# Two loads of W_v, and the normalisation of the last three tiles of x, moved earlier in a Strassen-blocked graph attention kernel

## The chip, the cores and the metric

One core of a Trainium2 chip runs the whole program. The metric is the device time of one execution in microseconds (us), and lower is better. The kernel before takes 630.65 us (median of three runs, 630.48 to 630.88). PE is the matrix engine, DVE the vector engine, ACT the scalar engine, POOL the GpSimd engine; SP issues most of the transfers. ACT and POOL issue transfers too.

## The reference, cut to what matters

The input has 2708 nodes with 1024 features, and a 0/1 adjacency matrix with about four ones in a row.

```
h = relu(layernorm(x))
q = h @ W_q.T + b_q;  k = h @ W_k.T + b_k;  v = h @ W_v.T + b_v
z = (q @ k.T) / 32 * adj;  z = where(z == 0, -10000, z)
out = x + relu(softmax(z, axis=1) @ v)
```

Everything is float32.

## The kernel before

**What is computed.** A row's scores are needed only where adj has a one. The program folds W_q and W_k into one matrix M of 1024x1024, forms a row q' = h M for each node, and takes the scalar products of q' with the few rows of h that adj names. The weighted sum u of these rows of h goes through W_v last: out = x + relu(u W_v.T + b_v). A rare general path (from L1397 on) is compiled but not run here.

**Stages.** (1) To about 104 us PE forms M. Meanwhile tiles of 128 rows of x are loaded, normalised and stored as `h_dram`, and DVE searches tiles of adj for their ones. (2) Ten "q pairs" (two row tiles each) are multiplied by M. Tiles 0 to 7, the early ones, are still in SBUF in their natural order. From tile 8 on the rows are gathered in an order sorted by number of neighbours; this needs the sorted table `tab` and all of `h_dram`. (3) The attention stream gathers neighbours' rows of h (`g`), multiplies them with q' on DVE (L863) and sums them (L923), tile after tile, beside stage 2 and 4. (4) Ten "o pairs" and one lone tile of u are multiplied by W_v.

**One pair.** A pair's product goes by Strassen's scheme in 512x512 blocks: seven products of eight matmuls each (`add_block`, L1010). The weights are M's four blocks, `M[:, i, j]`, and four combinations of them, `T[:, 0..3]`, which lie in the tile `wlow`. `multiply(n)` runs the pair's products with calls of `after(0)` to `after(6)` between them. All other work is issued from `after`. Between `after(5)` and the last product of pair n stands `between(n)`, which calls `opened(n + 1)`: it issues the first two products of the next pair, X with the weights `M[:, 0, 0]` (copied on to the bank Y by ACT at L1023) and Z with `T[:, 0]` for a q pair or `M[:, 0, 1]` for an o pair. So each pair is opened one pair ahead.

**From M to W_v.** With the last q pair (index 9, `last_q`) the weights change. Each block may be overwritten once its last q product has run. `b11` is `M[:, 0, 0]`, `t1` is `M[:, 0, 1]`, `b21` is `M[:, 1, 0]`. B11 of W_v goes to `M[:, 0, 0]`, and B22 to `T[:, 0]`, from where ACT copies it to `M[:, 1, 1]` (L1274) and where DVE takes it for `T[:, 1]` (L1282). The first o pair's X product needs B11.

**The early tiles' steps.** Strings of short steps, put at places (n, i) of `after` by the table `steps_at`, order the work of stage 2: `s8-10` loads x of tiles 8 to 10 and takes their moments on DVE (L237, L238), `r8` makes scale and shift of the three on POOL (nine small instructions, L259 to L267), `a8` normalises on ACT (L276), `k8` stores them to `h_dram` from ACT's queue (L283). `p` counts a tile of adj on ACT (L368), `f` searches one on DVE (L389), `w8-14 w15-21` writes the sorted table on POOL (L626), `z` reads it back (L638). At (2, 5) POOL adds tiles 8, 9 and 10 to `hsum` (L298, `owe`) and gathers the rows of the next two pairs (L612, tile `qr`). DVE and ACT run in the order in which the program issues, and POOL does so in this stretch.

**Queues.** Each engine issues its transfers in its own order, and an instruction that waits holds up all behind it on that engine.

Of the kernel before, what the change touches and what calls it, by code (L numbers as in the profile page):

```python
# [65 lines left out]
def tile_preln_masked_attention(  # L66
# [12 lines left out]
    nc = tc.nc  # L79
# [120 lines left out]
    M = core.tile([P, 2, 2, 4, NB], FT, name="M")  # L200
# [108 lines left out]
    def follow(steps):  # L309

        for step in steps.split():
            first, *only = step[1:].split(".")
            first, *last = first.split("-")
            first = int(first or 0)
            if step[0] == "s":
                stats(range(first, int(last[0] if last else first) + 1))
            elif step[0] == "m":
                moments(first)
            elif step[0] == "r":
                root(first)  # L320
            elif step[0] == "a":
                apply(first, *[range(int(o[0]), int(o[-1]) + 1) for o in only])
            elif step[0] in "hk":
                keep(first, step[0] == "h")
            elif step[0] == "+":
                owe(first)
            elif step[0] == "p":
                counted(first)
            elif step[0] == "c":
                counts(*halves[first])  # L330
            elif step[0] == "o":
                sorted_at.append(sort(*halves[first]))
            elif step[0] == "w":
                pooled.close()
                with tc.issue_after((behind if first < EARLY else products)[-1].ins):
                    entered.append(put(first, int(last[0]) + 1))
            elif step == "z":
                pooled.enter_context(tc.manual_schedule(engines={mybir.EngineType.Pool}))
                with tc.issue_after(entered[-1].ins):
                    reload(EARLY, NT)  # L340
            elif step[0] == "b":
                reload(*halves[first])
            elif step[0] == "g":
                squared(first)
            else:
                if step[0] == "e":
                    counted(first)
                if step[0] != "j":
                    found(first, *[range(int(o[0]), int(o[-1]) + 1) for o in only])
                if step[0] != "i":  # L350
                    listed(first)
# [81 lines left out]
    T = wlow.rearrange("p (k a) (b w) -> p k (a b) w", a=2, b=2)  # L433
# [12 lines left out]
    with tc.tile_pool(name="w", bufs=1, side="left") as wp:  # L446
# [11 lines left out]
        t1 = [work.tile([P, D], FT, tag="hT", name=f"t1_{k}", bufs=2) for k in range(2)]  # L458
# [145 lines left out]
    def small(name):  # L604
        return half.tile([P, NB], FT, tag="half", name=name, bufs=14)
# [157 lines left out]
    def natural_rows(n):  # L763
# [17 lines left out]

    steps_at = {(0, 0): "s4-5 p8 e9 +19 +20 +21", (0, 1): "r4 +0 +1 +2 i10.0-1", (0, 3): "p10", (0, 4): "i10.2-3 a4",
# [4 lines left out]
    steps_ahead = {(1, 5): "o1"}  # L787

# [219 lines left out]
    def add_block(bank, a, b, last=True):  # L1008
        for c in range(4):
            mm = nc.tensor.matmul(bank, a[:, c, :], b[:, c, :], start=False, stop=(c == 3), skip_group_check=True)  # L1010
        return mm
# [3 lines left out]
    def opened(n):  # L1015

        if n not in banks_of:
            return
        X, Z = banks_of[n]
        ops = ops_of[n][0]  # L1020
        add_block(X, ops["a11"], M[:, 0, 0])
        Y = psum.tile([P, NB], FT, tag="acc", name="psy")
        nc.scalar.copy(Y, X)  # L1023
        if n == FIRST:
            follow("o0")
        products.append(add_block(Z, ops["s1"], T[:, 0] if units[n][0] == "q" else M[:, 0, 1]))
        p5 = small("p5")
        nc.scalar.copy(p5, Z)
        opened_of[n] = Y, p5

    def between(n):

        if n == len(units) - 1:
            single["first"] = one_started(single["banks"], single["turned"][:, 0:4, :])
        else:
            opened(n + 1)

    def one_started(banks, a):

        X, Z = banks  # L1040
        add_block(X, a, M[:, 0, 0])
        first = small("p_single")
        nc.scalar.copy(first, X)
        return first

    def multiply(n, results, after):


        X, Z = banks_of.pop(n)
        ops = ops_of.pop(n)[0]  # L1050
        Y, p5 = opened_of.pop(n)
        after(0)
        after(1)
        products.append(add_block(Y, ops["s2"], T[:, 1]))
        u2 = small("u2")
        nc.scalar.copy(u2, Y)
        after(2)
        add_block(X, ops["a12"], M[:, 1, 0])
        results[0](X)
        after(3)  # L1060
        products.append(add_block(Z, ops["s4"], M[:, 1, 1]))
        results[2](Z, u2)
        after(4)
        products.append(add_block(Y, ops["s3"], T[:, 2]))
        results[1](Y, p5)
        after(5)
        between(n)
        add_block(Y, ops["a22"], T[:, 3])
        results[3](Y)
        after(6)  # L1070
# [119 lines left out]
    def of_wv(i, j):  # L1190

        return wv[j][:, i * 4:(i + 1) * 4, :]
# [26 lines left out]
    last_q = len(q_pairs) - 1  # L1219
# [13 lines left out]
    for n, unit in enumerate(units):  # L1233
# [15 lines left out]
        def after(i):  # L1249
# [15 lines left out]
                    with tc.issue_after(sorted_at[-1].ins):  # L1265
                        nc.vector.memset(g, 0.0)
            b11, t1, b21, b22 = M[:, 0, 0], M[:, 0, 1], M[:, 1, 0], M[:, 1, 1]
            for at, place, src in (((-2, 0), t1, of_wv(0, 0)), ((0, 0), T[:, 0], of_wv(1, 1)), ((0, 0), b11, of_wv(0, 0)),
                                   ((0, 3), b21, of_wv(1, 0))):
                if (n - last_q, i) == at:  # L1270
                    nc.sync.dma_start(place, src)
            if (n - last_q, i) == (0, 4):
# [302 lines left out]
```

## Time and profile before

| | |
|---|---|
| time, median of 3 | 630.65 us |
| the profiled execution, whole | 635.63 us |
| its span, first to last instruction | 633.9 us |
| PE busy | 623.0 us (98%) |
| DVE / POOL / ACT busy | 525.2 / 370.7 / 291.6 us |
| TensorE clock granted, mean | 0.994 |
| moved by DMA | 182.19 MB, mean 287 GB/s |

The profile is one execution on the chip with every instruction's start and duration. PE is busy nearly throughout, so what it waits for and how fast it is clocked set the time; the other engines matter where PE, or a chain that ends in PE, waits for them.

### The profile page before, as it was taken

The page shows a single profiled execution, that of the slowest core. Times are in us where ns is not written, and L with a number is a line of the kernel's source. Part 1 is how long each engine was busy: PE and PEld are TensorE (multiplying, and loading weights), DVE is VectorE, ACT ScalarE, POOL GpSimd, SP SyncE. Part 2 cuts the span into 40 slices and gives each one's busy share as a digit, 9 for nine tenths or more (in the row PEclk, how much of TensorE's full clock was granted, in tenths as well). Part 3 has the DMA queues.
Part 4 walks back from the last instruction along what each step waited for, and adds up shares of the span by engine and source line. Part 5 has one row for each costly group of instructions (what it writes and reads, how often), then busy time and mean ns, then how long its engine had stood idle before and what let it go on. Part 6 is the DMA issues. An engine that isn't in the chain of part 4 may idle for free.

```text
span 633.9 us, 6066 instructions
## 1 busy us (share of the span) xinstructions
PE 623.0 (98%) x1579; PEld 312.0 (49%) x1579; DVE 525.2 (83%) x1022; ACT 291.6 (46%) x421; POOL 370.7 (58%) x394
## 2 busy tenths in 40 slices
PE   9999999999998999999999989999999999999996
PEld 5777766444444544444444434444444444444442
DVE  5999879898897845899897879998988998988741
ACT  3538985749477372443332333444433324342300
POOL 2639960885766677666543432878566776762241
PEclk9999999999999999999999989999999999999999
DMA  8999997598788469996686999899999999996391
GB/s 333 407 365 316 340 351 301 207 320 307 262 257 337 135 196 369 296 410 191 207 343 197 362 346 305 261 335 318 330 285 344 291 297 307 341 286 172 102 295 71
DMA packets 65089, 182.19 MB, mean 287 GB/s; under 512 B 9960, under 2 KB 20024, under 8 KB 64409
## 3 DMA queue, kind: packets, MB, share of 16 engines
q0 software_dynamic: 26656, 86.02, 43.3%
q1 hardware_dynamic: 31594, 71.53, 32.7%
q10 hardware_dynamic: 6798, 24.20, 9.8%
q8 instruction: 14, 0.23, 0.2%
q14 instruction: 27, 0.21, 0.1%
HBM read 146.70 MB, written 43.36 MB: 300 GB/s over the span
## 4 chain that ended last, share of the span: by engine, by line
PE 96%; DMA 3%; issue 0%; POOL 0%; SPq 0%; DVE 0%; ACT 0%; POOLq 0%
PE ps L1010 44%; PE psy L1010 32%; PE ps_y L476 6%; PE ps_x L476 4%; PE ps_z L476 4%; PE pt L415 3%; DMA M<-in_wv_dram 2%; DMA qr<-h_dram,tab 1%; PE ps_y L511 1%; PE ps_h L1226 0%; PE ps_v L594 0%; DVE y_alone L1391 0%; POOL out_dram L1375 0%; ACT q L1101 0%; POOLq L1397 0%
## 5 line engine op out<-in xcount | busy, mean ns | idle before, releaser
L610 POOL DMA_INDIRECT g<-h_dram,tab x93 | 120.5, 1296 | 62.7 <-ACT u L912 21.7
L1010 PE MATMUL ps<-M,a 128*128 128x512 f32 x320 | 145.8, 599 | 2.0 <-DMA M<-in_wv_dram 2.0
L1010 PE MATMUL psy<-wlow,s 128*128 128x512 f32 x320 | 145.1, 596 | 0.0
L863 DVE SCALAR_TENSOR_TENSOR junk<-g,pq 128x1024 uint8<-128x1024 f32 x92 | 112.4, 1221 | 11.8 <-issue 4.9
L1010 PE MATMUL ps<-M,s 128*128 128x512 f32 x240 | 107.9, 592 | 0.0
L1010 PEld LDWEIGHTS ps<-M,a 128*128 128x128 f32 x320 | 60.4, 192 | 75.4 <-issue 71.2
L1010 PEld LDWEIGHTS psy<-wlow,s 128*128 128x128 f32 x320 | 60.6, 192 | 72.9 <-issue 71.9
L923 DVE SCALAR_TENSOR_TENSOR u<-g,coef,u 128x1024 f32<-128x1024 f32 x70 | 89.7, 1281 | 5.5 <-ACT u L912 4.0
L389 DVE FIND_INDEX8 at<-ones,adj 128x8 uint32<-128x685 f32 (+1 forms) x88 | 74.5, 865 | 0.0
L1010 PEld LDWEIGHTS ps<-M,s 128*128 128x128 f32 x240 | 45.5, 190 | 57.2 <-issue 56.5
L1010 PE MATMUL psy<-wlow,a 128*128 128x512 f32 x160 | 71.9, 592 | 0.0
L368 ACT ACTIVATE sized<-adj 128x2708 uint8<-128x2708 f32 (+1 forms) x22 | 54.2, 2465 | 7.9 <-DMA adj<-in_adj_dram 6.6
L1111 POOL DMA_INDIRECT y<-in_x_dram,tab x19 | 34.6, 1821 | 35.6 <-ACT y L1128 24.2
L298 POOL TENSOR_TENSOR hsum<-hsum,x 128x256 f32<-128x256 f32 (+1 forms) x56 | 38.8, 738 | 25.5 <-DVE wlow L444 21.4
L1010 PEld LDWEIGHTS psy<-wlow,a 128*128 128x128 f32 x160 | 30.4, 190 | 38.3 <-issue 37.1
L808 POOL DMA_INDIRECT out_dram<-y,tab x21 | 27.0, 1287 | 19.2 <-issue 13.1
L1010 PE MATMUL ps<-wlow,s 128*128 128x512 f32 x80 | 36.0, 593 | 0.0
L944 ACT COPY v<-u 128x1024 f32<-128x1024 f32 x19 | 19.8, 1044 | 29.1 <-DVE u L923 25.8
L760 ACT COPY ps<-bp_sb 128x512 f32<-128x512 f32 x42 | 24.6, 595 | 10.3 <-DVE y L1146 9.7
L626 POOL DMA_INDIRECT tab_dram<-tab,pos_i x22 | 21.7, 985 | 11.2 <-DVE pos_i L689 5.7
L276 ACT ACTIVATE x<-x,r 128x1024 f32<-128x1024 f32 (+1 forms) x22 | 25.8, 1232 | 5.2 <-POOL r L266 5.2
L912 ACT ACTIVATE u<-g,coef 128x1024 f32<-128x1024 f32 x16 | 18.4, 1149 | 21.3 <-DVE coef L911 13.2
(253 smaller groups left out, 843.4 us busy)
## 6 DMA issues: line engine op xcount, KB each, us to landing
adj<-in_adj_dram SPq DMA_DIRECT2D x21, 1354.0 KB
x<-in_x_dram SPq DMA_DIRECT2D x21, 512.0 KB
h_dram<-x ACTq DMA_DIRECT2D x21, 512.0 KB
u_dram<-v ACTq DMA_DIRECT2D x19, 512.0 KB
or<-u_dram SPq DMA_DIRECT2D x76, 128.0 KB
q_late<-q SPq DMA_DIRECT2D x12, 512.0 KB
pq<-q_late POOLq DMA_DIRECT2D x12, 512.0 KB
M<-in_wv_dram SPq DMA_DIRECT2D x3, 1024.0 KB
```

The source lines that it names most:

```text
L276: nc.scalar.activation(xs[i][:n], xs[i][:n], AF.Relu, bias=r[:n, 4, i:i + 1], scale=r[:n, 3, i:i + 1])
L298: small.append(nc.gpsimd.tensor_add(hsum[:n, cols], hsum[:n, cols], xt[:n, cols]))
L368: nc.scalar.activation(sized[:n], a[:n, :, :PW], AF.Abs, accum_out=total[:n, t:t + 1])
L389: nc.vector.max_index(at[:n, k - first_k, g, :], ones[:n, 0:8], a[:n, g, :])
L476: mm = nc.tensor.matmul(bank, a_tile(o + H * a[0], a[1], i), b(o), start=first and o == 0, stop=(o == H - 1), skip_group_check=True)
L610: return nc.gpsimd.indirect_dma_start(out=dst, out_offset=None, in_=src, in_offset=off, bounds_check=N - 1, oob_is_err=False)
L760: nc.scalar.copy(return_[h], row[:, h * NB:(h + 1) * NB])
L808: to = nc.gpsimd.indirect_dma_start(out=out, out_offset=bass.IndirectOffsetOnAxis(ap=ptab.bitcast(U32)[:n, t, SLOTS:SLOTS + 1], axis=0), i ...
L863: chained(lambda: nc.vector.scalar_tensor_tensor(junk, g_of[t][s], 1.0, tq[t], op0=ALU.mult, op1=ALU.mult, accum_out=zall[:, t, s:s + 1]))
L923: chained(lambda: nc.vector.scalar_tensor_tensor(u, g_of[t][s], coef[:, s:s + 1], u, op0=ALU.mult, op1=ALU.add))
L1010: mm = nc.tensor.matmul(bank, a[:, c, :], b[:, c, :], start=False, stop=(c == 3), skip_group_check=True)
L1111: return nc.gpsimd.indirect_dma_start(out=y[:n], out_offset=None, in_=x, in_offset=off, compute_op=ALU.add)
```

## The change

Two edits. **First**, B22 and B11 of W_v are loaded right behind `opened(last_q)`, in `between(last_q - 1)`, in place of `after(0)` of the last q pair, and B22 goes ahead of B11 as it did. **Second**, in `steps_at` the moments and the root of tiles 8 to 10 (`s8-10 r8`) go from (1, 5) to a place of their own, (1, 4), and their normalisation and stores (`a8 k8`) from (2, 3) to the head of (1, 5). No instruction is added or taken out.

```diff
                 (0, 5): "f11 p11 k4 s6-7", (0, 6): "+3 +4 f12 m6 m7", (1, 1): "p12 f13 c1 r6 +5", (1, 2): "p13",
-                (1, 3): "a6 k6 p14", (1, 5): "s8-10 w8-14 r8 w15-21 f14 f15", (1, 6): "f16 p15", (2, 1): "f17",
-                (2, 2): "p16", (2, 3): "p17 a8 k8 z", (2, 4): "p18", (2, 5): "f18 f19", (2, 6): "p19 f20 p20",
+                (1, 3): "a6 k6 p14", (1, 4): "s8-10 r8", (1, 5): "a8 k8 w8-14 w15-21 f14 f15", (1, 6): "f16 p15", (2, 1): "f17",
+                (2, 2): "p16", (2, 3): "p17 z", (2, 4): "p18", (2, 5): "f18 f19", (2, 6): "p19 f20 p20",
...
         else:
             opened(n + 1)
+        if n == last_q - 1:
+            nc.sync.dma_start(T[:, 0], of_wv(1, 1))
+            nc.sync.dma_start(M[:, 0, 0], of_wv(0, 0))
...
-            for at, place, src in (((-2, 0), t1, of_wv(0, 0)), ((0, 0), T[:, 0], of_wv(1, 1)), ((0, 0), b11, of_wv(0, 0)),
-                                   ((0, 3), b21, of_wv(1, 0))):
+            for at, place, src in (((-2, 0), t1, of_wv(0, 0)), ((0, 3), b21, of_wv(1, 0))):
                 if (n - last_q, i) == at:
                     nc.sync.dma_start(place, src)
```

SP's queue around the loads of W_v, in pairs 8 and 9, before (`wlow` is the tile of `T`, `or` the first o pairs' rows, `q_late` the store of q' of tiles 8 to 19):

```order
L1086 DMA q_late<-q_2152 128x1024
L700 DMA or_2258<-u_dram 32x4x256 x4
L700 DMA or_2263<-u_dram 32x4x256 x4
L1086 DMA q_late<-q_2153 128x1024
L1271 DMA wlow<-in_wv_dram 128x2048
L1271 DMA M<-in_wv_dram 128x2048 x2
L700 DMA or_2370<-u_dram 32x4x256 x4
```

and of the change:

```order
L1089 DMA q_late<-q_2152 128x1024
L700 DMA or_2258<-u_dram 32x4x256 x4
L700 DMA or_2263<-u_dram 32x4x256 x4
L1038 DMA wlow<-in_wv_dram 128x2048
L1039 DMA M<-in_wv_dram 128x2048
L1089 DMA q_late<-q_2153 128x1024
L1273 DMA M<-in_wv_dram 128x2048
L700 DMA or_2370<-u_dram 32x4x256 x4
```

B22 and B11 now stand ahead of the store of q' of tile 17; B21 stands where it stood.

DVE in pair 1, around the sort of the table (L682 to L689; `x_1110` and the two after it are tiles 8 to 10, which the change numbers `x_1094`, `x_1100`, `x_1106`), before:

```order
L1096 TENSOR_TENSOR q_992<-ps_880,u_1048 128x512
L1093 TENSOR_TENSOR q_993<-psy,p_957 128x512
L682 COPY sort<-ps_all 128x252
...
L689 CAST pos_i<-deg 128x14
L237 BN_STATS st<-x_1110 128x6 x2
L238 BN_AGGR mv<-st 128x2
L237 BN_STATS st<-x_1116 128x6 x2
L238 BN_AGGR mv<-st 128x2
L237 BN_STATS st<-x_1122 128x6 x2
```

and of the change:

```order
L1099 TENSOR_TENSOR q_992<-ps_880,u_1048 128x512
L237 BN_STATS st<-x_1094 128x6 x2
L238 BN_AGGR mv<-st 128x2
L237 BN_STATS st<-x_1100 128x6 x2
L238 BN_AGGR mv<-st 128x2
L237 BN_STATS st<-x_1106 128x6 x2
L238 BN_AGGR mv<-st 128x2
L1096 TENSOR_TENSOR q_993<-psy,p_957 128x512
L682 COPY sort<-ps_all 128x252
```

The moments of the three tiles now run ahead of the sort, and of the addition that stood before it. On POOL the nine small instructions of `r8`, which stood between the last writes of the table, accordingly stand ahead of all fourteen of these writes.

ACT between pair 1 and pair 2 (`sized` is a count of adj, `psy<-ps` the copy at L1023), before:

```order
L368 ACTIVATE sized,total<-adj_161 128x2708
L1023 COPY psy<-ps_1077 128x512
L1028 COPY p_1173<-ps_1079 128x512
L1101 COPY q_993<-psy 128x512
...
L368 ACTIVATE sized,total<-adj_161 128x2708
L276 ACTIVATE x_1110<-x_1110,r 128x1024
L276 ACTIVATE x_1116<-x_1116,r 128x1024
L276 ACTIVATE x_1122<-x_1122,r 128x1024
L283 DMA h_dram<-x_1110 128x1024
L283 DMA h_dram<-x_1116 128x1024
L283 DMA h_dram<-x_1122 128x1024
L368 ACTIVATE sized,total<-adj_157 128x2708
```

and of the change:

```order
L368 ACTIVATE sized,total<-adj_161 128x2708
L276 ACTIVATE x_1094<-x_1094,r 128x1024
L276 ACTIVATE x_1100<-x_1100,r 128x1024
L276 ACTIVATE x_1106<-x_1106,r 128x1024
L283 DMA h_dram<-x_1094 128x1024
L283 DMA h_dram<-x_1100 128x1024
L283 DMA h_dram<-x_1106 128x1024
L1023 COPY psy<-ps_1077 128x512
L1028 COPY p_1179<-ps_1079 128x512
L1104 COPY q_993<-psy 128x512
```

The three normalisations and their stores now stand one pair earlier, directly ahead of the copy of X to Y for pair 2. They no longer stand ahead of a count of adj in pair 2.

## Prediction

> **What bounds the kernel now.** The page comes first, for the engine that is never free, then the waits of that engine.
>
> ```profile
> PE 623.0 (98%) x1579; PEld 312.0 (49%) x1579; DVE 525.2 (83%) x1022; ACT 291.6 (46%) x421; POOL 370.7 (58%) x394
> PE pt L415 <- DMA qr<-h_dram,tab: 2.1, 1, 2.1
> PE ps L1010 <- DMA M<-in_wv_dram: 2.0, 1, 2.0
> ```
>
> PE sets the time. Behind the start it waits twice: for the first rows in sorted order (`qr`), and for B11 of W_v. The change aims at both. The chain of waits and the windows show that a gap costs more than its idle time.
>
> ```profile
> 202.98 1.54 PE pt L415 x8
> 204.53 4.64 PE psy L1010 x8
> 209.17 0.88 PE pt L415 x8
> 217.09 3.43 PE psy L1010 x8
> 366.93 8.80 PE ps L1010 x16
> 202.00:206.00 4.00, 3.02 (x10) 2.04 (x11) 3.76 (x17) 1.17 (x2) 4.00 (x7) 0.68 0.60 240
> 366.00:370.00 4.00, 3.07 (x4) 1.31 (x5) 2.26 (x3) 0.15 (x1) 2.38 (x2) 0.66 1.03 401
> ```
>
> Eight transposes take 0.88 us and eight matmuls 3.43 us, but right behind the gaps 1.54, 4.64, and 8.80 for sixteen; the granted clock there is 0.68 and 0.66 (the column behind the five engines). So gap A costs 2.1 + (1.54 - 0.88) + (4.64 - 3.43) = 4.0 us, and gap B 2.0 + (8.80 - 6.86) = 3.9. Together: 7.9.
>
> [...]
>
> **The gather (gap A).** What released it? POOL's rows, then ACT's:
>
> ```profile
> 186.65 5.54 POOL L298 TENSOR_TENSOR hsum<-hsum,x 128x256 f32<-128x256 f32 x8
> 197.56 1.08 POOL L612 DMA_INDIRECT qr<-h_dram,tab  x1 [5.38 <-PE ps L1010]
> 159.15 0.58 ACT L1023 COPY psy<-ps 128x512 f32<-128x512 f32 x1
> 182.88 2.36 ACT L276 ACTIVATE x<-x,r 128x1024 f32<-128x1024 f32 x2
> 185.28 1.47 ACTq L283 DMA_DIRECT2D h_dram<-x  x2
> 162.00:166.00 4.00, 4.00 (x17) 2.25 (x16) 3.97 (x12) 0.79 (x2) 3.09 (x4) 1.00 0.15 47
> 194.00:198.00 4.00, 4.00 (x11) 1.77 (x10) 2.10 (x5) 3.23 (x5) 0.43 (x1) 1.00 1.03 414
> ```
>
> The gather reads any row of `h_dram`, so it must wait for all stores. Of PE it needs only a free row buffer, that of tile 4, which was transposed for pair 2 a whole pair earlier; that a product ends just before 197.56 is then chance. The last stores leave ACT at 186.7, into a window in which the DMA engines are full (1.03, 414 GB/s). I take them as the releaser. Moved by a pair, they leave at about 163, where the engines are nearly idle (0.15).
>
> Then POOL itself is next: it reads back the table and adds to `hsum` until 186.65 + 5.54 = 192.2, so the gather starts at about 192.3. From gather to transposes it took 202.98 - 197.56 = 5.4 us; 192.3 + 5.4 = 197.7, and PE is free at 202.98 - 2.1 = 200.9. **Gap A closes with 3.2 us to spare**, if nothing upstream slips. Three places could.
>
> ```profile
> 154.39 0.69 DVE L1093 TENSOR_TENSOR q<-psy,p 128x512 f32<-128x512 f32 x1 [2.42 <-PE psy L1010]
> 159.71 1.23 DVE L237 BATCH_NORM_STATS2 st<-x 128x6 f32<-128x512 f32 x2
> 145.77 0.22 POOL L259 TENSOR_SCALAR r<-mv 128x2 f32<-128x2 f32 x1 [2.83 <-ACT junk_x L247]
> 148.74 0.22 POOL L267 TENSOR_SCALAR msq<-r 128x2 f32<-128x2 f32 x1
> 158.66 1.13 POOL L626 DMA_INDIRECT tab_dram<-tab,pos_i  x1 [3.03 <-DVE pos_i L689]
> 165.48 3.60 PE L1010 MATMUL psy<-wlow,s 128*128 128x512 f32 x8
> 199.40 0.09 DVE L389 MATCH_VALUE_LOAD at<-ones,adj 128x8 f32 x1 [3.30 <-DMA adj<-in_adj_dram]
> 210.26 1.28 DVE L722 TENSOR_TENSOR s<-a,pt 128x512 f32<-128x512 f32 x2 [0.36 <-ACT a L718]
> 213.44 1.93 PE L1010 MATMUL ps<-wlow,s 128*128 128x512 f32 x4
> ```
>
> *The table.* Moments of three tiles take 3 x 1.23 us of DVE and a little between them, some 3.9; 2.4 of them fill DVE's wait before 154.39, so the sort ends 1.5 us later, and the first write on POOL goes from 158.7 to 160.2. The root (nine instructions, 145.77 to 148.96: 3.2 us) runs from 155.9 to 159.1 and holds nothing up; the writes lose the steps between them, which I count as nothing. At worst the gather slips 1.5 us, half the margin.
>
> *ACT.* Normalising and storing took 182.88 to 186.75, 3.9 us. Started at 159.1 it ends at 163.0, and the copy at L1023 at 163.6. The product on Y wants it at 165.48: 1.9 us of cover. A root later than 161 would stall PE here, us for us.
>
> *The search.* With A gone PE is 4.0 us earlier, and DVE's last search sits close: from landing of the last adj tile (199.40) to `s` at L722 (210.9) go 11.5 us, and PE would want `s` at 213.44 - 4.0 = 209.4. So that tile must land 1.5 us sooner. Its buffer is freed by a count that stood behind the 3.9 us of ACT work now gone, and 1.57 MB of stores leave the full window, 3.8 us at 414 GB/s. Between nothing (a new gap of 1.5) and 3.9, I take 3: no gap.
>
> **W_v (gap B).** SP's rows, and what waited:
>
> ```profile
> 344.13 3.60 PE L1010 MATMUL ps<-wlow,s 128*128 128x512 f32 x8
> 351.81 0.34 SPq L1086 DMA_DIRECT2D q_late<-q  x1
> 352.25 0.38 SPq L1271 DMA_DIRECT2D wlow<-in_wv_dram  x1
> 352.95 5.44 SPq L1271 DMA_DIRECT2D M<-in_wv_dram  x2
> 350.00:354.00 4.00, 4.00 (x10) 1.71 (x9) 3.99 (x5) 1.42 (x3) 2.86 (x4) 1.00 0.88 263
> 359.75 1.15 POOL L833 DMA_DIRECT2D pq<-q_late  x2 [4.02 <-DMA q_late<-q]
> 364.17 2.29 DVE L1282 TENSOR_TENSOR wlow<-wlow,M 128x2048 f32<-128x2048 f32 x1 [1.71 <-DMA wlow<-in_wv_dram]
> 371.21 1.23 DVE L863 SCALAR_TENSOR_TENSOR junk<-g,pq 128x1024 uint8<-128x1024 f32 x1 [2.95 <-DMA pq<-q_late]
> ```
>
> B22 can go when the Z product ends at 347.7, B11 0.7 us later: 4.5 us sooner than 352.25 and 352.95. B11 landed at 366.8, 13.9 us from issue. With the same 13.9 it lands at 362.3; PE wants it at 366.93 - 2.0 = 364.9: 2.6 us of cover. The other bound, no gain because the gathers of that window hold the engines until 352, leaves gap B as it is; but they moved only 263 GB/s at 350 where 414 were seen, and a 0.5 MB store no longer stands ahead. I take the first. **Gap B closes.**
>
> The price is at tile 17's q', whose store (351.81) now queues behind 2 MB. In the trace it took 359.75 - 351.8 = 7.9 us to land, and the reload on POOL let DVE go on at 371.2. Call its delay D. Bounds: below, -2 (the engines are fuller earlier, so all of it ends sooner); above, the store lands 7.9 us behind B11's 362.3, at 370.2, D = 10.4. Same bytes, other order: I take D about 0. L1282 is ready sooner, and its 1.7 us only lengthen DVE's wait for q'.
>
> **Does the end follow?** The last rows stand behind all of DVE's stream.
>
> ```profile
> 390.59 0.69 DVE L722 TENSOR_TENSOR s<-a,s 128x512 f32<-128x512 f32 x1
> 396.17 3.60 PE L1010 MATMUL ps<-M,s 128*128 128x512 f32 x8
> DVE p L1123 <- ACT taken L1077: 3.9, 4, 1.6
> DVE u L1127 <- PE ps L1010: 3.6, 5, 1.2
> 609.07 1.25 DVE L705 STREAM_TRANSPOSE T_alone<-or 128x1024 f32<-128x1024 f32 x1 [10.76 <-DMA or<-u_dram]
> 610.78 3.60 PE L1010 MATMUL ps<-M,T_alone 128*128 128x512 f32 x8
> ```
>
> T_alone is ready at 610.3, 0.5 us ahead of PE: a PE that runs ahead of the stream would stop there. Gap A's share comes to the stream too, since it starts from the sort of the early tiles, whose counts come from PE (L680). For gap B's 4 us DVE must catch up: between 380 and 540 it waits 3.9 + 3.6 = 7.5 us for PE's results, and these waits shrink as PE gets earlier. 4 + D is below 7.5, so it does. On the way there is `s` at 391.3 against PE at 396.2: 4.9 us of cover, 0.9 - D left. No stall at D = 0.
>
> **The sum.** Span 633.9 - 4.0 - 3.9 = 626.0, and with the 1.73 us around it 627.7 against the profiled 635.63. The timed median is 4.98 us below that execution. A timed span cannot exceed 630.65, so at least 633.9 - 630.65 = 3.25 us of the profiled span are missing in timed runs; PE's products repeat at 3.43 us, and only gaps and ends can give way. If gaps alone do, timed runs hold 7.9 - 4.98 = 2.9 us of them; if half of the 1.73 is profiling too, 3.8. I take 3.8: **626.8 us**, likely between 625.5 and 628.
>
> **The rivals.**
> *The profile's surplus lies outside.* Then timed runs hold the whole 7.9: 622.75. Against it stands the span above 630.65; for it, that some of the span's end may be profiling. Chance 0.13. [...]
> *Only one gap goes*, say because PE did release the gather as its row reads, or `s` at 209.4 is late: half of 3.8, 628.7. Chance 0.12.
> *Nothing to be had*: new waits take it back, or timed runs have hardly a gap: 630.6. Chance 0.09.
> *Slower: the store behind 2 MB.* PE then stops at the product of 396.2 for D - 0.9, plus 1.9 at the low clock. That eats the 7.9 from D = 6.9. At the bound of 10.4 the gap is 9.5 + 1.9 = 11.4, net 3.5 slower: 634. For it: that store alone took 7.9 us. Against: at 350 the engines had room. Chance 0.06.
>
> **The numbers.** Main case 0.60. 0.2% is 1.3 us, about what a measurement of this kernel tells from no change. Faster 0.60 + 0.13 + most of 0.12 = 0.82; same 0.11; slower 0.07. The range goes from 622.4, just below the first rival, to 630.0; it leaves out the last two cases, 0.15, and a little below.
>
> **What would show it.** PE's waits without both rows, the clock at 1.00 in the windows of 202 and 366. The gather on POOL near 192, ACT's stores near 163 with L1023 done before 165.5. SP's load of B22 near 344 (347.7 less A's 4) and `q_late` behind it. T_alone's wait ending some 8 us sooner in the trace. Wrong would be a PE wait at L1010 for ACT near 165, for DVE near 209 or 392, or for T_alone near 603.

## The result, and the profile after

| | before | after |
|---|---|---|
| time, median of 4 runs | 630.57 us (630.23 to 630.88) | 636.75 us (635.98 to 638.91) |
| the profiled execution, whole / span | 635.63 / 633.9 us | 636.28 / 634.6 us |

After to before is 1.010 (95% interval 1.0085 to 1.0114). The forecast was 626.8 us, with 622.4 to 630.0 as its range: **the change made the kernel 1% slower, and the prediction was wrong in sign.**

The two profiled executions differ by 0.7 us only, the timed medians by 6.2. The profiled run of before was 5 us above its own median; so the kernel before was profiled a second time (run e0_before below), and that execution, 630.75 us with a span of 629.1, is the one to compare with. TensorE's waits, of the changed kernel:

```profile
PE 622.0 (98%) x1579; PEld 311.7 (49%) x1579; DVE 524.3 (83%) x1022; ACT 291.4 (46%) x421; POOL 367.6 (58%) x394
PE psy L1010 <- DVE q L1096: 5.4, 1, 5.4
PE ps_y L511 <- POOL hsum L121: 1.2, 1, 1.2
```

and of the kernel before in its second profile:

```profile
PE ps L1010 <- DMA M<-in_wv_dram: 1.8, 1, 1.8
PE ps_y L511 <- POOL hsum L121: 1.2, 1, 1.2
PE psy L1010 <- DVE q L1093: 0.9, 1, 0.9
```

Both rows that the change aimed at are gone after it, and a longer one has come. In the second profile of before there is no gap A at all, gap B is there, and the place of the new stop already shows with 0.9 us: the last product of the last q pair waits for the sum that VectorE makes for c22, the lower right block of the pair's result (L1093 before, L1096 after). The chain of waits leads back from there. Its columns are start, length, what. Before, second profile:

```profile
347.74 7.27 DMA q_late<-q
355.54 11.88 DMA pq<-q_late
368.71 1.23 DVE junk L863 x2
369.94 0.61 DVE q L1093
370.60 7.13 PE psy L1010 x16
```

After:

```profile
347.91 11.94 DMA q_late<-q
360.38 9.68 DMA pq<-q_late
371.34 1.23 DVE junk L863 x2
372.57 0.62 DVE q L1096
373.24 9.61 PE psy L1010 x16
```

The two run level until 347.7 and 347.9. Tile 17's q' is then stored, loaded again by POOL (`pq`), used by two scores, and behind these two VectorE makes the sum for c22. The product over the same bank must wait for that sum. From the store's issue to the reload's landing it took 367.4 - 347.7 = 19.7 us before and 370.1 - 347.9 = 22.2 us after. So TensorE goes on 2.6 us later. And its sixteen matmuls take 9.61 instead of 7.13 us, 2.5 more: behind the one stop of 5.4 us the granted clock falls to 0.50, behind the two stops of 1.8 and 0.9 us in e0_before it stays at 1.00:

```profile
370.00:372.00 2.00, 0.00 (x0) 0.86 1.06 337
372.00:374.00 2.00, 0.77 (x1) 0.50 1.03 334
374.00:376.00 2.00, 2.00 (x4) 0.50 1.04 337
376.00:378.00 2.00, 2.00 (x4) 0.50 0.97 386
378.00:380.00 2.00, 2.00 (x5) 0.94 0.25 100
```

(windows of the changed kernel: TensorE's busy time, the granted clock, the share of the DMA engines, GB/s). 2.6 + 2.5 = 5.1 of the 5.5 us between the spans 634.6 and 629.1. VectorE's rows of the changed kernel show the order that does it:

```profile
361.87 0.69 DVE L1099 TENSOR_TENSOR q<-ps,u 128x512 f32<-128x512 f32 x1
370.08 1.23 DVE L863 SCALAR_TENSOR_TENSOR junk<-g,pq 128x1024 uint8<-128x1024 f32 x1 [7.52 <-DMA pq<-q_late]
371.34 1.22 DVE L863 SCALAR_TENSOR_TENSOR junk<-g,pq 128x1024 uint8<-128x1024 f32 x1
372.49 0.69 DVE L1096 TENSOR_TENSOR q<-psy,p 128x512 f32<-128x512 f32 x1
```

### The profile page after: what moved, and what is told of

It reads as the page before. It is cut to its first block, busy times and chain, and to the rows that moved or that the text cites. A ratio compares the mean times of both kernels' runs of the same rounds, so it can differ in the third digit from the quotient of the medians.

```text
span 634.6 us, 6075 instructions
## 1 busy us (share of the span) xinstructions
PE 622.0 (98%) x1579; PEld 311.7 (49%) x1579; DVE 524.3 (83%) x1022; ACT 291.4 (46%) x421; POOL 367.6 (58%) x394
## 4 chain that ended last, share of the span: by engine, by line
PE 95%; DMA 3%; DVE 0%; issue 0%; POOL 0%; ACT 0%; POOLq 0%
PE ps L1010 43%; PE psy L1010 32%; PE ps_y L476 6%; PE ps_x L476 4%; PE ps_z L476 4%; PE pt L415 3%; DMA q_late<-q 2%; DMA pq<-q_late 2%; PE ps_y L511 1%; PE ps_h L1229 0%; PE ps_v L594 0%; DVE junk L863 0%; DVE y_alone L1393 0%; POOL out_dram L1377 0%; DVE q L1096 0%
## 5 line engine op out<-in xcount | busy, mean ns | idle before, releaser
L1010 PE MATMUL ps<-M,a 128*128 128x512 f32 x320 | 144.0, 593 | 0.0
L863 DVE SCALAR_TENSOR_TENSOR junk<-g,pq 128x1024 uint8<-128x1024 f32 x92 | 112.4, 1222 | 16.2 <-DMA pq<-q_late 7.5
L1010 PE MATMUL psy<-wlow,a 128*128 128x512 f32 x160 | 74.5, 610 | 5.4 <-DVE q L1096 5.4
L476 PE MATMUL ps_y<-wlow 128*128 128x512 f32 x64 | 27.6, 592 | 0.0
```

Of the source, the lines that this page charges most:

```text
L476: mm = nc.tensor.matmul(bank, a_tile(o + H * a[0], a[1], i), b(o), start=first and o == 0, stop=(o == H - 1), skip_group_check=True)
L863: chained(lambda: nc.vector.scalar_tensor_tensor(junk, g_of[t][s], 1.0, tq[t], op0=ALU.mult, op1=ALU.mult, accum_out=zall[:, t, s:s + 1]))
```

## The experiments

Two theories stood against each other at first. **Mine:** the new stop, behind tile 17's q', is the whole loss. **The rival:** the moved steps, or the executions that happened to be profiled, make it. Then, within mine: is it the place of the store behind 2 MB on one queue, or the throughput of the DMA engines? All ratios are to the kernel before on the same chip; it took 630.8 to 631.2 us beside three of the five groups of runs, and 634.5 and 635.0 beside the two others, on other chips.

### The kernel before again, each half alone, the change again

e0_before is the kernel before, unedited. e1_steps has only the new table of steps, e2_loads only the early loads:

```diff
 e2_loads: the table of before, and
+        if n == last_q - 1:
+            nc.sync.dma_start(T[:, 0], of_wv(1, 1))
+            nc.sync.dma_start(M[:, 0, 0], of_wv(0, 0))
```

> The kernel before, unchanged, as a second profile of it beside its own timed runs. The changed kernel's profiled run was 636.28 and its timed runs 635.98 to 638.91, while the kernel before was profiled at 635.63 and timed at 630.48 to 630.88. Theory (the stop that the change makes is new, and the profiled run of before was one of its longer executions): about 630.6 in all runs, a span near 628.9, and in the trace gap A (TensorE waiting for the gathered rows near 201) or gap B (waiting for W_v's blocks near 367) shorter than the 2.1 and 2.0 us of the first profile. Rival (profiled executions are longer by 5 us whatever the kernel): timed 630.6, profiled 635.6 again, with both gaps of 2 us.

> Only the first part of the change: the six steps of the table moved, W_v's blocks loaded where they were before. Theory: gap A closes, gap B stays, and nothing new comes: 1.4 to 4.0 us less than before, 626.6 to 629.2. Rival (the moved steps are what costs the time): slower than before, 632 to 637, with a stop of TensorE elsewhere than at 367 to 373 us.

> Only the second part: W_v's blocks B22 and B11 loaded early, the steps as before. Theory: gap A stays, gap B closes, and the last product of the last q pair waits about 5.4 us for VectorE's sum that stands behind the scores of tile 17, with some 6.8 us at half clock after it: slower than the changed kernel by the price of gap A, 637 to 641. Rival (the moved steps are what costs the time): 627 to 630, no stop above 2 us after 340 us.

> The changed kernel once more, as it is, beside the other runs on the same chip. Theory: 1.008 to 1.011 of the kernel before, with the one stop of 4.5 to 7 us at the last product of the last q pair. Rival (its loss hangs on the chip): within 0.3% of before.

| run | ratio, 95% | TensorE's stops in its profile |
|---|---|---|
| e0_before | 0.9999 (0.9989 to 1.0009) | 1.8 gap B, 0.9 sum |
| e1_steps | 1.0020 (1.0009 to 1.0032) | 1.6 gap B, 0.3 sum, 0.7 near 184 |
| e2_loads | 1.0077 (1.0060 to 1.0094) | 6.3 sum |
| e13_after | 1.0117 (1.0096 to 1.0137) | 6.1 sum, 2.0 near 185 |

The loads alone make most of the loss, as I expected, though their 636.18 us lie just below the 637 to 641 that I gave: there was no gap A whose price could be added. The moved steps alone, from which I expected a gain of 1.4 to 4.0 us, cost 0.2%, clear of no change. So the stop at the sum is not quite the whole loss: 0.8% and 0.2% make up the 1.0%. In e0_before gap A was not there to be closed. The gather has no gap behind it there, and its row names what I had argued for, the stores of `h_dram`, not TensorE:

```profile
193.12 1.08 POOL L612 DMA_INDIRECT qr<-h_dram,tab  x1 [2.42 <-DMA h_dram<-x]
200.63 1.04 PE L415 MATMUL pt<-ident,qr 128*128 128x128 f32 x8
```

193.1 there against 197.6 in the first profile. Counted over all profiles taken, gap A (1.7 to 2.6 us) is in 5 of 9 with the old table, and in none of 11 with the new one. But seven of these 11 have another stop instead, of 0.7 to 2.0 us between 178 and 186, which none of the 9 has. In e1_steps it is `s` for the next pair, behind a search whose tile of adj came late:

```profile
177.07 0.09 DVE L389 MATCH_VALUE_LOAD at<-ones,adj 128x8 f32 x1 [6.87 <-DMA adj<-in_adj_dram]
184.50 3.67 PE L1010 MATMUL ps<-wlow,s 128*128 128x512 f32 x8 [0.73 <-DVE s L722]
```

That tile's load was not held back: it left at 163.54, where in e0_before it left at 166.13. It took longer, 13.5 us until 177.07 instead of 8.5 us until 174.60. From 162 to 166 us the DMA engines moved 42 GB/s in e0_before (busy share 0.14) and 354 GB/s in e1_steps (1.02), where the three moved stores are issued from 161.0 to 163.6. That these stores make the load late is argued from these numbers; no run moves them alone.

### What makes the way of q' longer

e3_queue sends tile 17's store from ACT's queue. e5_b22 puts only B22 ahead of the store. e8_late moves B21's load, e12_no_loads leaves B22 and B11 out.

```diff
 e3_queue:
-            (nc.scalar if t < 4 else nc.sync).dma_start(dst, q)
+            (nc.scalar if t < 4 or t == BARE - 3 else nc.sync).dma_start(dst, q)
 e5_b22: in between() only T[:, 0]; b11 at ((0, 0), b11, of_wv(0, 0)) as before
 e8_late: b21 not at (0, 3), but
+            if (n - last_q, i) == (0, 5):
+                nc.scalar.dma_start(b21, of_wv(1, 0))
 e12_no_loads: the three lines in between() taken out
```

> The changed kernel, but tile 17's q' goes to memory from ScalarE's queue, so that it does not stand behind W_v's 2 MB on SyncE's queue. Theory (the order on one queue holds it back): the store lands some 8 us after its issue or sooner (11.9 in the changed kernel), q' is back near 366, the two scores end near 368.5 and the sum near 369.3; TensorE stops 1 to 2 us instead of 5.4, with one stretch of half clock instead of two: 630 to 633. Rival (the DMA engines' throughput holds it back, whatever the queue): 11 to 12 us from issue to landing again, a stop of 5 us, 636 to 638.

> The changed kernel with only one block (B22, 1 MB) ahead of tile 17's q' on SyncE's queue; B11 is loaded behind it, as before. Theory (each MB ahead of the store costs the path of q' its transfer): q' comes back between the 367.4 of the kernel before and the 370.1 of the changed one, near 368.5 to 369, and TensorE's stops together end 1 to 1.5 us sooner than the changed kernel's; if a part of them falls on B11's landing, no stop is longer than 2 us and the half clock goes too: 631 to 635. Rival (one load more or less ahead of the store makes no difference): 636 to 637.

> The changed kernel, but W_v's third block (B21, 1 MB) is asked for from ScalarE's queue some 7 us later in the same pair, so that it does not share the DMA engines with tile 17's q' on its way out and back. Theory (the way of q' is long because the DMA engines are full, whatever the queue): the way from the store's issue to the landing, 22.1 us in the changed kernel, takes about 20 us, TensorE stops some 3.4 us instead of 5.4 and still falls to half clock: 633.5 to 635.5. Rival (something else than shared throughput sets the way): 22 us again, 636 to 637.

> The changed kernel with W_v's blocks B22 and B11 not loaded at all, so that the products with W_v are formed with what lies in their places (the other two blocks are loaded as in the changed kernel): the 2 MB are taken out of the traffic. Theory (the DMA engines are full from 346 to 364 us, and every byte of the early loads comes out of the way of q'): 2.1 MB at some 420 GB/s are 5.0 us; the way from the store's issue to the landing takes 16 to 18.5 us, less than the 22.1 of the changed kernel and less than the 19.6 of the kernel before, VectorE hardly waits, TensorE does not stop at 367: 626 to 629 on a chip where before takes 630.6. Rival (the way is made of latencies): 19 us or more, and a stop of 2 us or more stays.

| run | the way of q', us | stop at the sum, us | ratio, 95% |
|---|---|---|---|
| before (e0_before) | 19.7 | 0.9 | 0.9999 |
| after | 22.2 | 5.4 | 1.010 |
| e3_queue | 369.5 - 347.7 = 21.8 | 5.0 | 1.0085 (1.0063 to 1.0107) |
| e5_b22 | 370.4 - 348.6 = 21.8 | 5.0 | 1.0081 (1.0055 to 1.0107) |
| e8_late | 374.3 - 350.2 = 24.1 | 7.3 | 1.0081 (1.0052 to 1.0111) |
| e12_no_loads | 365.7 - 349.5 = 16.2 | none | 0.9971 (0.9952 to 0.9990) |

The place on the queue is not it: on ACT's queue the store landed sooner (9.13 us instead of 11.94), but the reload took 12.09 instead of 9.68. With one block ahead it was the same (8.11 and 13.19). Here the times and stops of the rivals that I had written down were nearer than those of my theory. e8_late missed both: the store took 11.57 us, hardly less, and the reload 12.01, and TensorE stopped longer, 7.3 us; whether the block then met the reload was not shown. Of these four, only taking the 2 MB out shortens the way, to 16.2 us, the low end of what the throughput theory expected:

```profile
365.74 1.23 DVE L863 SCALAR_TENSOR_TENSOR junk<-g,pq 128x1024 uint8<-128x1024 f32 x1 [1.57 <-DMA pq<-q_late]
368.16 0.69 DVE L1093 TENSOR_TENSOR q<-psy,p 128x512 f32<-128x512 f32 x1
369.30 3.60 PE L1010 MATMUL psy<-wlow,a 128*128 128x512 f32 x8
```

The sum ends 0.5 us ahead of TensorE there. The queues' shares from 344 to 354 us (packets, MB, share of the 16 engines) say who paid; POOL's queue, with the gathers and the reload, is q0, SP's is q1. Before, second profile:

```profile
q0 software_dynamic: 723, 2.64, 75.5%
q1 hardware_dynamic: 164, 0.73, 17.7%
```

After:

```profile
q1 hardware_dynamic: 263, 2.01, 55.3%
q0 software_dynamic: 406, 1.47, 43.2%
```

The engines were busy in both (93.2% and 98.5%). What SP's queue moves 4 us sooner, POOL's queue moves later: 1.2 MB of gathers. The six gathers issued in this window took 8.1 us from issue to landing before and 16.6 after (medians). And the reload lands late whenever the store lands: the store landed at 359.9 in the changed kernel, 356.8 in e3_queue and 356.7 in e5_b22, the reload at 370.1, 369.5 and 370.4. The two queues' shares of the 16 engines moved against each other: SP's rose from 17.7% to 55.3%, POOL's fell from 75.5% to 43.2%. And the store on ACT's queue (e3_queue) won 0.6 us of the reload's landing only. That the gathers ahead of the reload, rather than the reload itself, carry the delay is argued from these numbers. They do not give its size: in e5_b22 POOL's queue still moved 2.02 MB in the same 10 us, and the way was as long as in e3_queue, where it moved 1.32.

### The consumer moved

e4_order and e6_loads_order put the sum for c22 ahead of the two scores on VectorE, with the whole change and with the loads alone; e7_before_order does so in the kernel before.

```diff
-            if n > FIRST:
-                advance(share)
+            if n > FIRST and (n, i) != (last_q, 4):
+                advance(share * (2 if (n, i) == (last_q, 5) else 1))
```

> The changed kernel, but in the last q pair VectorE's sum for c22 (L1096) stands ahead of the two scores that wait for tile 17's q', not behind them; the loads and the store stay as the change has them. Theory (TensorE stops only because of that order): q' comes back as late as in the changed kernel, near 370, and VectorE still waits for it, but TensorE does not: the 5.4 us and the 2.7 us of half clock behind it go, 628 to 629. Rival (what comes behind the late scores on VectorE is needed as soon, so that the stop only moves on): a stop of 2 to 4 us at a later product, near 388 to 396 us, 631 to 634.

> The early loads and VectorE's new order, with the table of steps as it was before. Theory: no stop at 340 to 380 us, and no gap A either, since the two profiles of the kernel before show that stop in one execution and not in the other: 627.5 to 628.5, some 3 us faster than before. Rival (the stop only moves on): 631 to 634.

> The kernel before with only VectorE's new order: the loads at their old place. Theory: the 1.8 us that TensorE waits for B11 stay, the 0.9 us that it waits for the sum behind the scores go: 630.0 to 630.5, 0.7 to 1 us faster than before. Rival (the 0.9 us are hidden behind another wait): no change, 630.9 to 631.3.

The ratios were 1.0047 (1.0031 to 1.0064), 1.0025 (1.0011 to 1.0039) and 1.0004 (0.9993 to 1.0015). TensorE's longest waits in e6_loads_order:

```profile
PE ps L1010 <- DVE T_alone L705: 1.4, 1, 1.4
PE ps_y L511 <- POOL hsum L121: 1.2, 1, 1.2
PE psy L1010 <- ACT u L1059: 1.0, 1, 1.0
```

and VectorE there:

```profile
362.27 0.68 DVE L1096 TENSOR_TENSOR q<-psy,p 128x512 f32<-128x512 f32 x1
370.09 1.23 DVE L863 SCALAR_TENSOR_TENSOR junk<-g,pq 128x1024 uint8<-128x1024 f32 x1 [7.14 <-DMA pq<-q_late]
```

The stop at the sum is gone and the half clock with it (mean granted clock 0.997, in e2_loads 0.994): from 1.0077 to 1.0025. So the order on VectorE turned the late q' into TensorE's stop. But it was not "only because of that order", as I had it: VectorE still idles 7.1 us where e0_before has 3.3 and falls behind by that. As I read it, TensorE meets the delay at a later product, behind ACT, and again at the last tile. Here the rival came true (634.22 and 631.91 us), with smaller stops than it gave, none above 2.0. In e7_before_order the 0.9 us go from the profile, but of the 0.7 to 1 us that I gave no gain can be told in the time.

### A shorter way

e9_direct, e10_loads_direct and e11_before_direct copy tile 17's q' from SBUF to SBUF on POOL's queue in place of store and reload: with the whole change, with the loads alone, and in the kernel before. e14_direct_order adds the new order on VectorE to e9_direct, e15_direct2_order also copies tile 18. e16_fix_no_steps is e15_direct2_order with the old table, e17_fix_no_loads with old table and old places of the loads.

```diff
-            nc.gpsimd.dma_start(tq[t], q_late[(t - EARLY) * P:(t - EARLY + 1) * P, :])
+            nc.gpsimd.dma_start(tq[t], kept[t] if t in kept else q_late[(t - EARLY) * P:(t - EARLY + 1) * P, :])
...
-            (nc.scalar if t < 4 else nc.sync).dma_start(dst, q)
+            if t == BARE - 3:
+                kept[t] = q
+            else:
+                (nc.scalar if t < 4 else nc.sync).dma_start(dst, q)
```

> The changed kernel, but tile 17's q' is copied from one SBUF tile to the other by one DMA, and not stored to memory and loaded again: one transfer of 0.5 MB and one landing less. Theory (the stop is that way's length and nothing else): q' is there some 10 to 12 us after it is formed, near 358 to 360, VectorE does not wait for it, TensorE does not stop at 367, and the half clock goes: 627.5 to 629.5, faster than before. Rival (VectorE's own work, not the way of q', is then what TensorE waits for): stops of 1 to 2 us further on, 630 to 632.

> As the run before it, with the table of steps as it was before: the early loads and the copy from SBUF to SBUF. Theory: as that run or up to 1 us less, since the moved steps gave 1.002 by themselves: 627.0 to 629.0. Rival (VectorE's own work sets the end): 630 to 631.

> The kernel before with only the copy from SBUF to SBUF for tile 17: the loads at their old place, now without a store ahead of them on SyncE's queue. Theory: the 0.9 us at the last product go, and B11 lands up to 1 us sooner, so that 0.8 to 1.8 us of its stop stay: 628.5 to 630.2. Rival (the copy competes with the loads as the store did): B11 as late as before, 630.0 to 630.5.

> The changed kernel with tile 17's q' copied from SBUF to SBUF and with VectorE's sum for c22 ahead of the scores that wait. Theory: the 0.6 us that were left at the last product with the copy alone go, nothing else changes: 0.995 to 0.998 of before, 628 to 629.5 on a chip where before takes 630.6. Rival (VectorE, which still waits some 3 us for its rows, is the bound): as the copy alone, 0.997 to 0.999.

> As the run before it, with tile 18's q' copied from SBUF to SBUF as well: another 0.5 MB of store and one landing less. Theory: tile 18's rows are not what VectorE waits for by then, so the same as the run before it within 0.2%. Rival (the DMA engines are still the bound past 370 us): 0.3% faster than that run.

> The fastest version so far (early loads, the copies from SBUF to SBUF for tiles 17 and 18, VectorE's sum ahead of the scores) with the table of steps as before. Theory (gap A comes only in some executions, and the moved steps gave 1.002 by themselves): 0.995 to 0.997 of before, within 0.2% of the version with the moved steps. Rival (gap A is there in most runs on this chip): 0.3 to 0.6% slower than that version.

> The kernel before with the copies and the new order alone, W_v's blocks at their old place. Theory (once q' comes back in time, the early loads are worth gap B, 1.8 us): 0.3% slower than the run beside it, 0.998 to 1.000 of before. Rival (the early loads are worth nothing even then): the same as the run beside it within 0.1%.

| run | loads early | steps moved | time, us | before, us | ratio, 95% |
|---|---|---|---|---|---|
| e9_direct | yes | yes | 631.86 | 634.45 | 0.9973 (0.9946 to 1.0000) |
| e10_loads_direct | yes | no | 632.00 | 634.45 | 0.9960 (0.9942 to 0.9978) |
| e11_before_direct | no | no | 632.45 | 634.45 | 0.9977 (0.9956 to 0.9998) |
| e14_direct_order | yes | yes | 629.32 | 631.02 | 0.9977 (0.9959 to 0.9994) |
| e15_direct2_order | yes | yes | 628.39 | 631.02 | 0.9964 (0.9950 to 0.9977) |
| e16_fix_no_steps | yes | no | 631.84 | 635.02 | 0.9954 (0.9937 to 0.9971) |
| e17_fix_no_loads | no | no | 632.46 | 635.02 | 0.9963 (0.9943 to 0.9983) |

The copy turns the changed kernel from 1.010 to 0.997: with q' back at 366.4 instead of 370.1, the loss is gone. It is not back at 358 to 360, as expected, though, and VectorE still waits 2.8 us for it. The chain of waits of e9_direct:

```profile
349.38 16.99 DMA pq<-q
```

One copy of 0.5 MB took 17 us. In e10_loads_direct the copy landed at 367.97 and the score started at 368.07, and its wait is put down to the gathered rows:

```profile
DVE junk L863 <- DMA g<-h_dram,tab: 3.0, 1, 3.0
```

So POOL's queue delivered neither before 366 to 368. Two expectations of e11_before_direct failed: the wait for the sum grew to 1.7 us (the score starts at 371.01, again behind the gathers), and of B11's wait nothing stayed. TensorE's waits in e15_direct2_order, the fastest version on the chip where before takes 631.02 us:

```profile
PE ps_y L511 <- POOL hsum L121: 1.2, 1, 1.2
PE ps L1010 <- DVE T_alone L705: 0.2, 1, 0.2
```

Nothing is left of either gap: 631.02 - 628.39 = 2.6 us. The new order beside the copy (e14_direct_order) and the copy of tile 18 lie within the intervals of the versions without them. What each half of the change adds to the copy stays open too: e16_fix_no_steps and e17_fix_no_loads lie within the intervals of each other, and of e17_fix_no_loads the rival was nearer than my theory, by which it should have been 0.3% slower.

But neither e17_fix_no_loads nor e11_before_direct is a test of late loads. On SP's queue W_v's blocks had waited behind tile 17's store, and that store behind ACT's copy of tile 17's q' (until 347.7 in e0_before). Without a store there they leave 0.2 us behind the product that frees their place (in e17_fix_no_loads 346.96 against 346.77) and not 4.5 us as in e0_before (348.18 against 343.66). The copy thus makes the loads early by itself, and gap B is gone in both runs. A copy with late loads was not run, so the gain belongs to the two together.

## Why the prediction was wrong, point by point

**Gap A: mechanism right, size wrong.** The gather was forecast for 192.3 and started at 192.37, ACT's copy (L1023) was forecast to end at 163.6 and ended at 163.97, and the row buffer's release by TensorE was rightly called chance. That the gather came within 0.1 us is partly luck: POOL had issued the read-back of the table by 185.8 instead of 186.65, and its additions then waited 0.9 us for the next copy of ACT's at L1023, a wait that I had not counted. And the 4.0 us were taken from one long execution. In e0_before the gather starts at 193.1, and 5.4 us on, at 198.5, it is 2.1 us ahead of TensorE (200.6), and the gap is worth nothing. The three places that could slip did not include the stop near 185 that came: I had called the new place of the stores, near 163, nearly idle, and a tile of adj is loaded just there.

**Gap B: closes, as forecast.** B22 left at 343.86 (forecast 344), T1 (L1284) no longer waits. This step held.

**The delay D: the sum's mis-sized term.** I took D at about 0, within bounds of -2 and 10.4. The score behind the reload starts at 370.08. In the first profile it starts at 371.21, which is 367.3 without the 3.9 us of gap A, so D measured 2.8 us; against e0_before it is 2.6. "Same bytes, other order" was the false sentence: the engines were full from 344 to 354 us (93.2% in e0_before, 98.5% after), and what went earlier on SP's queue took the place of the gathers on POOL's (2.64 MB before, 1.47 after). The bounds held; e3_queue and e5_b22 show that the term is not the wait behind 2 MB from which I had built the upper one.

**"Does the end follow?": the step that failed.** I looked for the first product that could miss q' and named `s` at 396.2, with 4.9 us of cover. The first consumer stood 20 us earlier. In the very profile that I had read, the reload lets VectorE go at 371.21, two scores follow, then L1093 ends at 374.3, and the product on its bank starts at 375.57:

```profile
373.63 0.69 DVE L1093 TENSOR_TENSOR q<-psy,p 128x512 f32<-128x512 f32 x1
375.57 3.60 PE L1010 MATMUL psy<-wlow,a 128*128 128x512 f32 x8
```

That is 1.3 us of cover, against 7.9 us by which I made TensorE earlier. Gap A moves both sides by 3.9, gap B only TensorE. So even with D = 0 TensorE would have asked for the sum at 367.7 and got it at 370.4, a stop of 2.7 us, with or without a fall of the clock behind it (2.36 us had one in e11_before_direct, 2.62 us none in e10_loads_direct); with D = 2.8 it is 5.5, as measured (5.4). Gap B's wait was hiding another one right behind it.

**The slower rival: right in kind, wrong in place and price.** It said that the store behind 2 MB delays q' until TensorE stops, from D = 6.9. At the true consumer the stop is D + 2.7, so it decides from D = -2.7. Its 0.06 was far too little.

**What timed runs hold.** I argued for 2.9 to 3.8 us of gaps in them. e0_before shows 1.8 + 0.9 = 2.7 without any half clock, and the fastest version won 2.6. The rival with the surplus outside the span falls: e0_before lies 1.65 us above its span and the first profile 1.73; that one was a longer execution. That half of the 1.73 us is profiling, which the 3.8 assumed, no run shows.

## What to carry to other kernels

When a wait is to be removed, ask for every input of the next few instructions of the waiting engine when it comes, and what stands ahead of it on the engine that makes it: here the next wait in line set the gain. The sum for c22 had 1.3 us of cover in one profile and was already waited for, 0.9 us, in the other. The loads moved earlier here while the DMA engines were full (93.2% busy before, 98.5% after) were paid for by POOL's queue, whose gathers took 16.6 us to land instead of 8.1; look whose transfers share those microseconds and who waits for them. Look also at what else starts in a place that seems idle: the one near 163 us had a busy share of 0.14 in e0_before and 1.02 with the stores there, and the load of an adj tile took 13.5 us instead of 8.5. And profile the kernel before twice before pricing its gaps: gap A was 2.1 us in one profile and absent in the other.

## What the runs showed of the hardware

**A gap's length alone did not tell whether the clock fell.** Rows of TensorE behind gaps, of e4_order, e13_after, e11_before_direct and e10_loads_direct in turn:

```profile
386.48 3.70 PE L1010 MATMUL psy<-wlow,s 128*128 128x512 f32 x8 [1.98 <-ACT u L1059]
```

```profile
185.76 5.37 PE L1010 MATMUL ps<-wlow,s 128*128 128x512 f32 x8 [2.00 <-DVE s L722]
```

```profile
203.67 1.06 PE L415 MATMUL pt<-ident,qr 128*128 128x128 f32 x8 [2.36 <-DMA qr<-h_dram,tab]
204.57 5.30 PE L1010 MATMUL psy<-wlow,s 128*128 128x512 f32 x8
```

```profile
203.34 1.06 PE L415 MATMUL pt<-ident,qr 128*128 128x128 f32 x8 [2.62 <-DMA qr<-h_dram,tab]
204.24 3.60 PE L1010 MATMUL psy<-wlow,s 128*128 128x512 f32 x8
```

Behind 1.98 us the eight matmuls take 3.70 us at a granted clock of 1.00. Behind 2.00 and 2.36 us eight of them take 5.37 and 5.30, and the clock falls to 0.56 and 0.50 in windows of 2 us. Behind 2.62 us they take 3.60 at 1.00. Six gaps of 5.0 to 7.3 us cost 1.5 to 3.1 us of low clock each (from the start of the product behind the gap to that of the next, less 3.43). What decides whether a gap has this price was not shown.

**One copy of 0.5 MB took 17.0 us** (e9_direct) behind a queue of gathers on full DMA engines (busy share 0.99 to 1.05 from 349 to 367 us). A copy that skips memory was no remedy for the queue.

**Chips differ.** The same kernel before took 630.8 and 635.0 us on two chips; gap A was in all four profiles of the old table taken on the two slower ones, and in none of the four on the two faster ones; the chip of the first profile, which has it, is not known. Why they differ is open.
